# Regrouping the TensorE steps of a sliding-window attention stage, with the zeroed keys made on GpSimd

## The chip, the cores and the metric

The kernel runs on one core of one Trainium2 chip. The metric is the device time of one execution in microseconds (us). An execution of this kernel was also profiled; its lines are quoted as the profile has them.

## The reference

A block of three stages on x of shape (8, 512, 512) in float32: x plus half of a gated feed-forward network of layernorm(x), then x plus attention of layernorm(x), then the feed-forward step again. The change lies in the attention. It has 32 heads of 16 columns, and a query sees its own position and the 128 before it:

```
q, k, v = heads(x @ Wq.T), heads(x @ Wk.T), heads(x @ Wv.T)
scores = einsum('bhnrd,bhncd->bhnrc', qb, kw) * scale      # blocks of 128 queries, 256 keys
scores = where(valid, scores, finfo.min)                   # 0 <= dist <= 128, no key before 0
out = einsum('bhnrc,bhncd->bhnrd', softmax(scores), vw)
return out @ Wo.T
```

The softmax subtracts each query's largest visible score before it exponentiates, and the kernel does so too.

## The kernel before, in words

The kernel has three stages, one after the other: feed-forward "a" (`ffn_stage`), attention (`attention_stage`, tiles with "_b"), feed-forward "c". Tiles of rows pass between them through DRAM (`rows_a`, `rows_b`).

**Units.** The attention is cut into 128 units. Unit u stands for one row b of the batch (8), one group i of 8 heads (4 per row, j = i mod 4; i runs from 0 to 31) and one block t of 128 positions (4 per group). So a row has 16 units and a group four, t = 0 to 3. Eight heads of 16 columns fill 128 partitions, in four strips g of 32 partitions with two heads h in each.

**Steps of a unit, by function, line and tile name:**

- `probabilities` (L510): transposed scores, keys against queries, into four PSUM tiles `sp` (L519), one for each strip, as matmuls on 32 of TensorE's rows. Each tile is 128 x 512 with both heads and 256 queries, at t = 3 half as wide. The keys come from `kz`, two copies of the keys in each of which one head's columns are zero and one column is 1, and the queries carry minus the maximum in the matching column. Each tile is then clamped at zero into `pT` in SBUF, three of them by ScalarE (L532) and the last, g = 3, by VectorE (L528); ScalarE exponentiates the whole (L534), and GpSimd zeroes what lies outside the window (`affine_select`, L539).
- `weighted` (L545), one unit later: probabilities times values into PSUM tile `av` (L555), on 32 of TensorE's columns, 32 matmul instructions, 16 at t = 0. After every second unit ScalarE copies it to `ab` (L564).
- `turned` (L566), after every second unit: four transposes of `ab` to `abT` (L573), then on VectorE the reciprocal of the sums (L576) and four multiplications to `o` (L580).
- `turned_back` (L587): two transposes `oTp` (L592), copied to `oT` by ScalarE (L595).
- `maxima` (L475), six units ahead (AHEAD): scores once more, queries against keys, into four PSUM tiles `sm` (L487), 128 wide at t = 0 and 256 else; VectorE masks each and takes its largest, eight reductions (L496) into `negs`.
- `subtract` (L501), once per group: four transposes `neg` (L505), and two operations on VectorE (L508) that put the maxima into the queries.
- one product per unit of 128 x 512, eight matmul instructions at L431: `values` (wv, t = 0, for the next row; evacuated by VectorE, L467), `output` (wo, t = 1, for the row before; it adds the residual `xr`, L601 to L607), `queries` (wq, t = 2) and `keys` (wk, t = 3), both three groups ahead, evacuated by ScalarE (q: L449 and L450; k: L457; `kz`: L459 and L460).
- `norm` of row b + 2 (L174): its load by `row_loaded`, statistics, scaled rows `xn`, and four transposes `ptn` (L205), copied to `xs` by ScalarE (L213).

**Buffers.** `ps_s` has five PSUM banks, taken in turn by `sp` and `sm` tiles, so that a group of four tiles takes one bank that has been free and the first three banks of the group before. `ps_mm` has two, taken in turn by products and by all transposes; `ps_av` has one. `pT` has three buffers.

**Order.** The loop over u at the end of `attention_stage` is the order in which TensorE, VectorE and ScalarE take the attention's instructions (`manual_schedule`). On TensorE a unit is: `sp`, half of the product, (`neg`, or `abT` at odd u), `sm`, the product's other half, (`ptn`), `av`, (`oTp`). `sum_of_products` returns a function that is called once for each half:

```
            if product:
                product()
...
            if product:
                product()
```

GpSimd and SyncE aren't ordered by hand. SyncE issues the loads and stores, ScalarE the stores of the feed-forward stages.

Of the kernel before, what the change touches and what calls it, by code (L numbers as in the profile page):

```python
# [8 lines left out]
F32 = mybir.dt.float32  # L9
# [15 lines left out]
def macaron_block(  # L25
# [147 lines left out]
    def norm(xnpool, xspool, psum, tag, xt, split, name):  # L173
# [9 lines left out]

        def statistics(_=0):
            for t in range(TB):
                st = small.tile([P, 6], F32, tag="st", name=f"st_{name}_{t}")
                nc.vector.bn_stats(st, xt[:, t, :])
                nc.vector.bn_aggr(mv[:, t, :], st)
            var = small.tile([P, TB], F32, tag="nvar", name=f"var_{name}")
            nc.vector.tensor_scalar(var, mv[:, :, 1], LN_EPS, None, ALU.add)  # L190
            inv_sqrt(rstd, var)

# [95 lines left out]
    def ffn_stage(kind, source, target, first):  # L288
        with ExitStack() as s:
# [25 lines left out]
            def prepare(b):  # L315
                xts[b] = xpool.tile([P, TB, D], F32, tag="x", name=f"x_{kind}{b}")
                nc.sync.dma_start(xts[b], source(b))
                xss[b], statistics, scaled, transposed = norm(
                    xnpool, xspools[b % 2], ps_tr, "tr", xts[b], True, f"{kind}{b}"
                )  # L320
                with tc.high_priority() if b == 0 else nullcontext():
                    statistics()
                    for t in range(TB):
                        scaled(t)
                        transposed(t)
# [44 lines left out]
    def attention_stage():  # L370
# [42 lines left out]

        qs, ks, kz, pTs, avs, abs_, os_, oTs = {}, {}, {}, {}, {}, {}, {}, {}
        NJ = DC
# [5 lines left out]
        def sum_of_products(name, pairs, done):  # L421

            half = len(pairs) // 2
            box = []

            def part():
                first = not box
                if first:
                    box.append(ps_mm.tile([P, T], F32, tag="mm", name=name))
                for n in range(0 if first else half, half if first else len(pairs)):  # L430
                    nc.tensor.matmul(  # L431
                        box[0], *pairs[n], start=(n == 0), stop=(n == len(pairs) - 1)
                    )
                if not first:
                    done(box[0])

            return part

        def project(w, b, j, done):
            cols = slice(j * P, (j + 1) * P)  # L440
            pairs = [(attn_w[w][:, k, cols], xss[b][:, k, :]) for k in range(DC)]
            return sum_of_products(f"{w}_{b}_{j}", pairs, done)

        def queries(i):
            return project("wq", i // NJ, i % NJ, lambda ps: queries_kept(i, ps))

# [5 lines left out]
        def keys(i):  # L452
            return project("wk", i // NJ, i % NJ, lambda ps: keys_kept(i, ps))

        def keys_kept(i, ps):
            ks[i] = ring.tile([P, T], F32, tag="k", name=f"k_{i}", bufs=3)
            nc.scalar.copy(ks[i], ps)  # L457
            kz[i] = [ring.tile([P, T], F32, tag=f"kz{h}", name=f"kz{h}_{i}") for h in range(2)]
            nc.scalar.activation(kz[i][0], ps, AF.Identity, scale=half0, bias=at16)  # L459
            nc.scalar.activation(kz[i][1], ps, AF.Identity, scale=half1, bias=at0)  # L460

        def values(b, t):
            rows = slice(t * P, (t + 1) * P)
            pairs = [(xss[b][:, k, rows], attn_w["wv"][:, k, :]) for k in range(DC)]
            return sum_of_products(
                f"wv_{b}_{t}", pairs,
                lambda ps: nc.vector.tensor_copy(  # L467
                    vones[b % 2][:, t, :, :DK], ps.rearrange("p (h d) -> p h d", d=DK)
                ),
            )  # L470
# [39 lines left out]
        def probabilities(u):  # L510
# [14 lines left out]
            for g in range(NG):  # L525
                under = pT[:, 2 * g : 2 * g + 2, : n * P]
                if g == NG - 1:
                    nc.vector.tensor_scalar(  # L528
# [37 lines left out]
        def turned(u):  # L566

            i, t = u // TB, u % TB
            pt = ps_mm.tile([P, 2, 2, P], F32, tag="mm", name=f"abT_{u}")
            ab = abs_.pop(i)  # L570
            for m in range(2):
                for h in range(2):
                    nc.tensor.transpose(pt[:, m, h, :], ab[:, h, m, :], ident)  # L573
            rows = pt.rearrange("p m h (g r) -> p (m h) g r", r=32)
            rden = small.tile([P, 4, NG, 1], F32, tag="rden", name=f"rden_{u}")
# [9 lines left out]
        def turned_back(u):  # L585
# [11 lines left out]
            )  # L597

        def output(b, t):
            xr = work.tile([P, D], F32, tag="xr", name=f"xr_{b}_{t}")  # L600
            nc.sync.dma_start(xr, rows_a[b][:, t, :])  # L601
            rows = slice(t * P, (t + 1) * P)
# [5 lines left out]

            return sum_of_products(f"wo_{b}_{t}", pairs, done)

        AHEAD = 6
        row = NJ * TB
        engines = {mybir.EngineType.PE, mybir.EngineType.DVE, mybir.EngineType.Activation}
        s.enter_context(tc.manual_schedule(engines=engines))
        for u in range(-row - row // 2 - 2, units + row):
            i, t = u // TB, u % TB
            b, j = i // NJ, i % NJ
            if j == 1 and t == 2 and 0 < b + 2 < B:
                row_loaded(b + 2)
            if b == -2 and j == 2:  # L620
                with tc.high_priority():
                    for part in norms[0] if t == 0 else norms[0][1:]:
                        part(t)
            if j == 2 and t == 0 and 0 < b + 2 < B:
                norms[b + 2][0]()
            if 0 <= u < units:
                probabilities(u)
            product = None
            if b == -1 and j >= 2 and t < 2:
                product = values(0, 2 * (j - 2) + t)  # L630
            if t == 0 and 0 < b + 1 < B:
                product = values(b + 1, j)
            if t == 1 and 0 <= b - 1 < B:
                product = output(b - 1, j)
            if t == 2 and 0 <= i + 3 < B * NJ:
                product = queries(i + 3)
            if t == 3 and 0 <= i + 3 < B * NJ:
                product = keys(i + 3)
            if product:
                product()  # L640
            if j == 2 and 0 < b + 2 < B:
                norms[b + 2][1](t)
            if 0 <= u - 1 + AHEAD < units and (u - 1 + AHEAD) % TB == TB - 1:
                subtract((u - 1 + AHEAD) // TB)
            if 0 <= u - 2 < units and (u - 2) % 2 == 1:
                turned(u - 2)
            if 0 <= u + AHEAD < units:
                maxima(u + AHEAD)
            if product:
                product()  # L650
            if j == 2 and 0 < b + 2 < B:
                norms[b + 2][2](t)
            if 0 <= u - 1 < units:
                weighted(u - 1)
            if 0 <= u - 2 < units and (u - 2) % 2 == 1:
                turned_back(u - 2)
        s.close()

# [31 lines left out]
```

## Time and profile before

| | us |
|---|---|
| median of 3 runs | 2540.91 |
| lowest, highest | 2538.38, 2542.39 |
| the profiled execution's own time | 2538.64 |
| its span in the profile | 2536.9 |
| TensorE busy (PE) | 2446.1 |
| VectorE busy (DVE) | 1300.1 |
| ScalarE busy (ACT) | 1024.5 |
| GpSimd busy (POOL) | 895.5 |

In the profile PE is TensorE's matmuls and PEld its weight loads, which overlap them. A line of the timeline has the start in us, the length in us, the engine, the line of the kernel, the operation, output <- inputs, their shapes, how often, and in square brackets how long the engine was idle before it and what ended that. Matmuls are pipelined: their ends overlap the next step's start, so what a step costs is read from start to start. A matmul of float32 is two instructions in the profile, so `sp` shows as x16 and half a product as x4. A stretch line has from:to and length, then busy time and instructions of PE, PEld, DVE, ACT and POOL, the granted clock, the DMA share and GB/s. The feed-forward stages take the time up to about 829 us and from about 1803 us on; the units of the attention begin with the first `sp` at 877.0 us.

### The profile page before, as it was taken

The numbers are of one execution on the slowest core, as the hardware profiler recorded it, in microseconds if no ns is written. First come the engines' busy times: TensorE is split into PE (matmuls) and PEld (weight loads), VectorE is DVE, ScalarE is ACT, GpSimd is POOL, SyncE is SP. The second block draws the span as 40 slices with busy tenths as digits, with TensorE's granted clock in tenths as the row PEclk, the third lists the DMA queues.
The fourth block names the chain that finished last, engine by engine and source line by source line (L and its number), as shares of the span: only waits on it lengthen the run. The fifth ranks groups of instructions, "written<-read, shape, count | busy, mean of one in ns | idle before, by whom it ended". The sixth has DMA issues, their size and how long they took to land.

```text
span 2536.9 us, 40366 instructions
## 1 busy us (share of the span) xinstructions
PE 2446.1 (96%) x16184; PEld 1755.5 (69%) x16184; DVE 1300.1 (51%) x3785; ACT 1024.5 (40%) x1524; POOL 895.5 (35%) x742
## 2 busy tenths in 40 slices
PE   5789999999999999999999999999999999999998
PEld 4668888888888455555555555555688888888887
DVE  7774434434434465656665666666334433443433
ACT  6762222222222366666566565556322222222221
POOL 0004444444445132222222222223344444444444
PEclk9999999999999999999999999999999999999999
DMA  4431000000011000101010000013400000000000
GB/s 149 149 133 46 34 15 20 34 34 1 34 67 67 34 2 26 35 18 35 22 37 20 18 18 18 18 55 114 137 18 17 34 34 1 34 34 1 34 17 17
DMA packets 38907, 103.25 MB, mean 41 GB/s; under 512 B 2880, under 2 KB 6976, under 8 KB 35648
## 3 DMA queue, kind: packets, MB, share of 16 engines
q1 hardware_dynamic: 33344, 83.90, 9.6%
q10 hardware_dynamic: 5376, 16.78, 1.7%
q8 instruction: 127, 2.08, 0.3%
q14 instruction: 60, 0.49, 0.1%
HBM read 62.91 MB, written 37.75 MB: 40 GB/s over the span
## 4 chain that ended last, share of the span: by engine, by line
PE 90%; DVE 6%; ACT 2%; issue 1%; DMA 0%; POOL 0%; DVEq 0%; POOLq 0%; ACTq 0%; SPq 0%
PE gu_c L233 18%; PE gu_a L233 18%; PE o_c L266 9%; PE o_a L266 8%; PE sm L487 5%; PE sp L519 5%; PE wq L431 5%; PE wk L431 5%; PE wv L431 5%; PE wo L431 4%; PE av L555 4%; PE abT L573 1%; PE oTp L592 1%; DVE xn_a L197 1%; PE neg L505 1%
## 5 line engine op out<-in xcount | busy, mean ns | idle before, releaser
L233 PE MATMUL gu_a<-xs_a,wgu_a 128*128 128x512 f32 x2048 | 503.4, 398 | 14.8 <-ACT wgu_a L153 14.8
L233 PE MATMUL gu_c<-xs_c,wgu_c 128*128 128x512 f32 x2048 | 489.0, 391 | 0.0
L539 POOL TENSOR_SCALAR_AFFINE_SELECT pT<-pT 128x1024 f32<-128x1024 f32 x224 | 239.9, 1091 | 650.5 <-ACT pT L534 650.5
L233 PEld LDWEIGHTS gu_a<-xs_a,wgu_a 128*128 128x128 f32 x2048 | 388.7, 192 | 97.5 <-ACT wgu_a L153 17.4
L233 PEld LDWEIGHTS gu_c<-xs_c,wgu_c 128*128 128x128 f32 x2048 | 383.0, 188 | 78.7
L496 DVE CUSTOM_DVE_ANT_0 seen<-sm,window 128x256 f32<-128x256 f32 (+1 forms) x1024 | 330.9, 387 | 75.9 <-PE sm L487 66.8
L266 PE MATMUL o_a<-wp_a,hs_a 128*128 128x512 f32 x1024 | 254.0, 391 | 5.9 <-ACT wp_a L153 5.9
L266 PE MATMUL o_c<-wp_c,hs_c 128*128 128x512 f32 x1024 | 251.5, 389 | 0.0
L241 DVE TENSOR_TENSOR h_c<-gu_c,sg_c 128x512 f32<-128x512 f32 x128 | 88.5, 691 | 293.8 <-PE gu_c L233 291.5
L259 POOL TENSOR_TENSOR sq_c<-h_c 128x512 f32<-128x512 f32 x120 | 124.8, 1040 | 323.5 <-DVE h_c L241 309.8
L266 PEld LDWEIGHTS o_a<-wp_a,hs_a 128*128 128x128 f32 x1024 | 191.0, 188 | 46.9 <-ACT wp_a L153 7.8
L534 ACT ACTIVATE pT<-pT 128x2048 f32<-128x2048 f32 (+1 forms) x128 | 217.2, 1697 | 12.1 <-DVE pT L528 8.4
L266 PEld LDWEIGHTS o_c<-wp_c,hs_c 128*128 128x128 f32 x1024 | 192.3, 188 | 39.8
L241 DVE TENSOR_TENSOR h_a<-gu_a,sg_a 128x512 f32<-128x512 f32 x128 | 88.4, 691 | 256.0 <-PE gu_a L233 254.6
L259 POOL TENSOR_TENSOR sq_a<-h_a 128x512 f32<-128x512 f32 x105 | 109.7, 1045 | 276.5 <-DVE h_a L241 265.1
L532 ACT ACTIVATE pT<-sp 128x512 f32<-128x512 f32 (+1 forms) x384 | 181.2, 545 | 57.9 <-PE sp L519 57.9
L260 POOL TENSOR_TENSOR ss_c<-ss_c,sq_c 128x512 f32<-128x512 f32 x120 | 191.7, 1598 | 8.9
L239 ACT ACTIVATE sg_c<-gu_c 128x512 f32<-128x512 f32 x128 | 76.6, 598 | 270.2 <-PE gu_c L233 270.1
L243 ACT CAST hs_c<-h_c 128x512 fp32r<-128x512 f32 x128 | 79.6, 622 | 254.7 <-DVE h_c L241 254.7
L239 ACT ACTIVATE sg_a<-gu_a 128x512 f32<-128x512 f32 x128 | 76.6, 598 | 257.7 <-PE gu_a L233 257.7
L243 ACT CAST hs_a<-h_a 128x512 fp32r<-128x512 f32 x128 | 79.6, 622 | 225.2 <-DVE h_a L241 225.2
L260 POOL TENSOR_TENSOR ss_a<-ss_a,sq_a 128x512 f32<-128x512 f32 x105 | 167.6, 1596 | 7.8
(129 smaller groups left out, 3041.0 us busy)
## 6 DMA issues: line engine op xcount, KB each, us to landing
x_a<-x_dram SPq DMA_DIRECT2D x8, 1024.0 KB, 5.4
wf_gu<-w_gate_up_dram SPq DMA_DIRECT2D x16, 512.0 KB, 3.6
wgu_kept<-wgu_a SPq DMA_DIRECT2D x16, 512.0 KB, 2.8
rows_a<-x_a ACTq DMA_DIRECT2D x8, 1024.0 KB, 3.9
xr<-rows_a SPq DMA_DIRECT2D x32, 256.0 KB, 3.1
x_b<-rows_a SPq DMA_DIRECT2D x8, 1024.0 KB, 4.8
rows_b<-xr SPq DMA_DIRECT2D x32, 256.0 KB, 2.4
x_c<-rows_b SPq DMA_DIRECT2D x8, 1024.0 KB, 4.8
```

What stands on the lines that cost most here:

```text
L233: nc.tensor.matmul(ps, wgu[c][:, i * DC + k, :], xs[:, s, k, :], start=(k == 0 and s == 0), stop=(k == DC - 1 and s == 1),)
L239: nc.scalar.activation(sg, gu[0], AF.Silu)
L241: nc.vector.tensor_tensor(h, gu[1], sg, ALU.mult)
L243: nc.scalar.copy(hs[c][:, 0, :], h)
L259: nc.gpsimd.tensor_tensor(sq, h, h, ALU.mult)
L260: nc.gpsimd.tensor_tensor(sumsq, sumsq, sq, ALU.add)
L266: nc.tensor.matmul(ops[t], ht[:, s, t * P : (t + 1) * P], wp[e // 2][:, e % 2, :], start=(e == 0 and s == 0), stop=(e == FC - 1 and s == 1),)
L431: nc.tensor.matmul(box[0], *pairs[n], start=(n == 0), stop=(n == len(pairs) - 1))
L496: nc.vector.tensor_tensor_reduce(out=seen[:, : n * P], in0=tiles[g][:, h, : n * P], in1=window[:, (2 - n) * P :], scale=-1.0, scalar=3.4e3 ...
L532: nc.scalar.activation(under, tiles[g][:, :, : n * P], AF.Relu, scale=-1.0)
L534: nc.scalar.activation(seen, seen, AF.Exp, scale=-1.0)
L539: nc.gpsimd.affine_select(out=half, in_=half, compare_op=ALU.is_ge, fill=0.0, base=0, pattern=[[0, 2 * NG], [sign, P]], channel_multiplier ...
```

## The change

- The product of a unit is no longer cut in halves: `sum_of_products` issues all of it.
- The order of a unit on TensorE becomes: `sp`, `av` of the unit before, `sm`, (`neg`), the whole product, (`ptn`), then `abT` at even u and `oTp` at odd u. `turned` keeps the transposes, one unit earlier than before; its VectorE part becomes `divided`, which stands right after `probabilities`.
- The clamp that VectorE does is that of strip g = 1 in place of the last.
- The two `kz` tiles of a group are made by GpSimd from `k` in SBUF, one in each of the two units that follow `keys`, in place of by ScalarE from PSUM. GpSimd's order is now set by hand too.
- The residual rows are loaded one unit ahead of `output`, by ScalarE's queue in place of SyncE's.
- `row_loaded` stands at the end of j = 0, t = 3 in place of j = 1, t = 2, and the norm's statistics are spread over the four units of j = 1. On VectorE the norm's scaling now stands behind the unit's maxima.

```diff
@@ -181,14 +181,14 @@
         mv = small.tile([P, TB, 2], F32, tag="mv", name=f"mv_{name}")
         rstd = small.tile([P, TB], F32, tag="nrstd", name=f"rstd_{name}")
 
-        def statistics(_=0):
-            for t in range(TB):
-                st = small.tile([P, 6], F32, tag="st", name=f"st_{name}_{t}")
-                nc.vector.bn_stats(st, xt[:, t, :])
-                nc.vector.bn_aggr(mv[:, t, :], st)
-            var = small.tile([P, TB], F32, tag="nvar", name=f"var_{name}")
-            nc.vector.tensor_scalar(var, mv[:, :, 1], LN_EPS, None, ALU.add)
-            inv_sqrt(rstd, var)
+        def statistics(t):
+            st = small.tile([P, 6], F32, tag="st", name=f"st_{name}_{t}")
+            nc.vector.bn_stats(st, xt[:, t, :])
+            nc.vector.bn_aggr(mv[:, t, :], st)
+            if t == TB - 1:
+                var = small.tile([P, TB], F32, tag="nvar", name=f"var_{name}")
+                nc.vector.tensor_scalar(var, mv[:, :, 1], LN_EPS, None, ALU.add)
+                inv_sqrt(rstd, var)
 
         xns = {}
 
@@ -411,7 +412,8 @@
         for tile_ in negs:
             nc.gpsimd.memset(tile_, 0.0)
 
-        qs, ks, kz, pTs, avs, abs_, os_, oTs = {}, {}, {}, {}, {}, {}, {}, {}
+        later, xrs = [], {}
+        abTs, qs, ks, kz, pTs, avs, abs_, os_, oTs = {}, {}, {}, {}, {}, {}, {}, {}, {}
         NJ = DC
         units = B * NJ * TB
 
@@ -419,30 +421,18 @@
             return u // TB // NJ, u // TB % NJ, u % TB
 
         def sum_of_products(name, pairs, done):
-
-            half = len(pairs) // 2
-            box = []
-
-            def part():
-                first = not box
-                if first:
-                    box.append(ps_mm.tile([P, T], F32, tag="mm", name=name))
-                for n in range(0 if first else half, half if first else len(pairs)):
-                    nc.tensor.matmul(
-                        box[0], *pairs[n], start=(n == 0), stop=(n == len(pairs) - 1)
-                    )
-                if not first:
-                    done(box[0])
-
-            return part
+            ps = ps_mm.tile([P, T], F32, tag="mm", name=name)
+            for n, (lhs, rhs) in enumerate(pairs):
+                nc.tensor.matmul(ps, lhs, rhs, start=(n == 0), stop=(n == len(pairs) - 1))
+            done(ps)
 
         def project(w, b, j, done):
             cols = slice(j * P, (j + 1) * P)
             pairs = [(attn_w[w][:, k, cols], xss[b][:, k, :]) for k in range(DC)]
-            return sum_of_products(f"{w}_{b}_{j}", pairs, done)
+            sum_of_products(f"{w}_{b}_{j}", pairs, done)
 
         def queries(i):
-            return project("wq", i // NJ, i % NJ, lambda ps: queries_kept(i, ps))
+            project("wq", i // NJ, i % NJ, lambda ps: queries_kept(i, ps))
 
         def queries_kept(i, ps):
             qs[i] = [ring.tile([P, T], F32, tag=f"q{h}", name=f"q{h}_{i}") for h in range(2)]
@@ -450,19 +440,22 @@
             nc.scalar.activation(qs[i][1], ps, AF.Copy, scale=scale1)
 
         def keys(i):
-            return project("wk", i // NJ, i % NJ, lambda ps: keys_kept(i, ps))
+            project("wk", i // NJ, i % NJ, lambda ps: keys_kept(i, ps))
 
         def keys_kept(i, ps):
             ks[i] = ring.tile([P, T], F32, tag="k", name=f"k_{i}", bufs=3)
             nc.scalar.copy(ks[i], ps)
-            kz[i] = [ring.tile([P, T], F32, tag=f"kz{h}", name=f"kz{h}_{i}") for h in range(2)]
-            nc.scalar.activation(kz[i][0], ps, AF.Identity, scale=half0, bias=at16)
-            nc.scalar.activation(kz[i][1], ps, AF.Identity, scale=half1, bias=at0)
+            kz[i] = {}
+            later.extend([(i, 0, half0, at16), (i, 1, half1, at0)])
+
+        def keys_of_head(i, h, kept, at):
+            kz[i][h] = ring.tile([P, T], F32, tag=f"kz{h}", name=f"kz{h}_{i}")
+            nc.gpsimd.tensor_scalar(kz[i][h], ks[i], kept, at, ALU.mult, ALU.add)
 
         def values(b, t):
             rows = slice(t * P, (t + 1) * P)
             pairs = [(xss[b][:, k, rows], attn_w["wv"][:, k, :]) for k in range(DC)]
-            return sum_of_products(
+            sum_of_products(
                 f"wv_{b}_{t}", pairs,
                 lambda ps: nc.vector.tensor_copy(
                     vones[b % 2][:, t, :, :DK], ps.rearrange("p (h d) -> p h d", d=DK)
@@ -524,7 +517,7 @@
 
             for g in range(NG):
                 under = pT[:, 2 * g : 2 * g + 2, : n * P]
-                if g == NG - 1:
+                if g == 1:
                     nc.vector.tensor_scalar(
                         under, tiles[g][:, :, : n * P], -1.0, 0.0, ALU.mult, ALU.max
                     )
@@ -566,12 +559,15 @@
         def turned(u):
 
             i, t = u // TB, u % TB
-            pt = ps_mm.tile([P, 2, 2, P], F32, tag="mm", name=f"abT_{u}")
+            pt = abTs[i] = ps_mm.tile([P, 2, 2, P], F32, tag="mm", name=f"abT_{u}")
             ab = abs_.pop(i)
             for m in range(2):
                 for h in range(2):
                     nc.tensor.transpose(pt[:, m, h, :], ab[:, h, m, :], ident)
-            rows = pt.rearrange("p m h (g r) -> p (m h) g r", r=32)
+
+        def divided(u):
+            i, t = u // TB, u % TB
+            rows = abTs.pop(i).rearrange("p m h (g r) -> p (m h) g r", r=32)
             rden = small.tile([P, 4, NG, 1], F32, tag="rden", name=f"rden_{u}")
             nc.vector.reciprocal(rden, rows[:, :, :, DK : DK + 1])
             os_[i] = work.tile([P, 2, NG, 2, DK], F32, tag="o", name=f"o_{u}", bufs=2)
@@ -596,9 +592,12 @@
                 oTs[i][:, (t - 1) * P : (t + 1) * P], back.rearrange("p m q -> p (m q)")
             )
 
+        def residual_loaded(b, t):
+            xrs[b, t] = work.tile([P, D], F32, tag="xr", name=f"xr_{b}_{t}")
+            nc.scalar.dma_start(xrs[b, t], rows_a[b][:, t, :])
+
         def output(b, t):
-            xr = work.tile([P, D], F32, tag="xr", name=f"xr_{b}_{t}")
-            nc.sync.dma_start(xr, rows_a[b][:, t, :])
+            xr = xrs.pop((b, t))
             rows = slice(t * P, (t + 1) * P)
             pairs = [(oTs[NJ * b + j][:, rows], attn_w["wo"][:, j, :]) for j in range(NJ)]
 
@@ -606,54 +605,60 @@
                 nc.vector.tensor_tensor(xr, ps, xr, ALU.add)
                 nc.sync.dma_start(rows_b[b][:, t, :], xr)
 
-            return sum_of_products(f"wo_{b}_{t}", pairs, done)
+            sum_of_products(f"wo_{b}_{t}", pairs, done)
 
         AHEAD = 6
         row = NJ * TB
-        engines = {mybir.EngineType.PE, mybir.EngineType.DVE, mybir.EngineType.Activation}
+        engines = {
+            mybir.EngineType.PE, mybir.EngineType.DVE, mybir.EngineType.Activation,
+            mybir.EngineType.Pool,
+        }
         s.enter_context(tc.manual_schedule(engines=engines))
         for u in range(-row - row // 2 - 2, units + row):
             i, t = u // TB, u % TB
             b, j = i // NJ, i % NJ
-            if j == 1 and t == 2 and 0 < b + 2 < B:
-                row_loaded(b + 2)
             if b == -2 and j == 2:
                 with tc.high_priority():
-                    for part in norms[0] if t == 0 else norms[0][1:]:
+                    if t == 0:
+                        for block in range(TB):
+                            norms[0][0](block)
+                    for part in norms[0][1:]:
                         part(t)
-            if j == 2 and t == 0 and 0 < b + 2 < B:
-                norms[b + 2][0]()
             if 0 <= u < units:
                 probabilities(u)
-            product = None
-            if b == -1 and j >= 2 and t < 2:
-                product = values(0, 2 * (j - 2) + t)
-            if t == 0 and 0 < b + 1 < B:
-                product = values(b + 1, j)
-            if t == 1 and 0 <= b - 1 < B:
-                product = output(b - 1, j)
-            if t == 2 and 0 <= i + 3 < B * NJ:
-                product = queries(i + 3)
-            if t == 3 and 0 <= i + 3 < B * NJ:
-                product = keys(i + 3)
-            if product:
-                product()
-            if j == 2 and 0 < b + 2 < B:
-                norms[b + 2][1](t)
+            if 0 <= u - 2 < units and (u - 2) % 2 == 1:
+                divided(u - 2)
+            if later:
+                keys_of_head(*later.pop(0))
+            if 0 <= u - 1 < units:
+                weighted(u - 1)
+            if t == 0 and 0 <= b - 1 < B:
+                residual_loaded(b - 1, j)
+            if 0 <= u + AHEAD < units:
+                maxima(u + AHEAD)
+            if j in (1, 2) and 0 < b + 2 < B:
+                norms[b + 2][j - 1](t)
+
             if 0 <= u - 1 + AHEAD < units and (u - 1 + AHEAD) % TB == TB - 1:
                 subtract((u - 1 + AHEAD) // TB)
-            if 0 <= u - 2 < units and (u - 2) % 2 == 1:
-                turned(u - 2)
-            if 0 <= u + AHEAD < units:
-                maxima(u + AHEAD)
-            if product:
-                product()
+            if b == -1 and j >= 2 and t < 2:
+                values(0, 2 * (j - 2) + t)
+            if t == 0 and 0 < b + 1 < B:
+                values(b + 1, j)
+            if t == 1 and 0 <= b - 1 < B:
+                output(b - 1, j)
+            if t == 2 and 0 <= i + 3 < B * NJ:
+                queries(i + 3)
+            if t == 3 and 0 <= i + 3 < B * NJ:
+                keys(i + 3)
             if j == 2 and 0 < b + 2 < B:
                 norms[b + 2][2](t)
-            if 0 <= u - 1 < units:
-                weighted(u - 1)
+            if 0 <= u - 1 < units and (u - 1) % 2 == 1:
+                turned(u - 1)
             if 0 <= u - 2 < units and (u - 2) % 2 == 1:
                 turned_back(u - 2)
+            if j == 0 and t == 3 and 0 < b + 2 < B:
+                row_loaded(b + 2)
         s.close()
 
     ffn_stage("a", lambda b: tokens(x, b), lambda b: rows_a[b], True)
```

More of the change, by code (lines that the diff above doesn't have):

```diff
@@ L321, in prepare @@
                 with tc.high_priority() if b == 0 else nullcontext():
-                    statistics()
+                    for t in range(TB):
+                        statistics(t)
                     for t in range(TB):
```

## The prediction

> **What bounds the kernel now.** I read the page's busy shares first, then the busy time by stretch, then TensorE's timeline of a steady group, then the one place where TensorE is seen to wait for score banks.
>
> ```profile
> PE 2446.1 (96%) x16184; PEld 1755.5 (69%) x16184; DVE 1300.1 (51%) x3785; ACT 1024.5 (40%) x1524; POOL 895.5 (35%) x742
> ...
> PE 90%; DVE 6%; ACT 2%; issue 1%; DMA 0%; POOL 0%; DVEq 0%; POOLq 0%; ACTq 0%; SPq 0%
> ```
>
> TensorE carries nine tenths of the chain. By stretch (length, then busy time of PE, PEld, DVE, ACT, POOL):
>
> ```profile
> 1341.10:1459.10 118.00, 116.83 (x1169) 64.23 (x1168) 73.67 (x341) 71.44 (x106) 30.99 (x29) 1.00 0.06 19
> 1577.10:1692.10 115.00, 115.00 (x1156) 62.25 (x1155) 68.59 (x328) 69.30 (x102) 29.98 (x28) 1.00 0.06 20
> ```
>
> These are two rows b (16 units each) of the attention stage, the only stage the change touches in time: rows take 118.0 us with the norm of a later row inside, 115.0 without. TensorE never rests in the second. Two units (t = 2, then the start of t = 3) on TensorE:
>
> ```profile
> 1355.48 1.15 PE L519 MATMUL sp<-q,kz 32*128 32x256 f32 x16
> 1356.56 1.99 PE L431 MATMUL wq<-xs_b,wq_sb 128*128 128x512 f32 x4
> 1358.38 0.60 PE L505 MATMUL neg<-ident,negs 128*128 128x128 f32 x4
> 1358.91 0.73 PE L487 MATMUL sm<-k,q 32*128 32x128 f32 x16
> 1359.57 1.98 PE L431 MATMUL wq<-xs_b,wq_sb 128*128 128x512 f32 x4
> 1361.48 1.08 PE L555 MATMUL av<-pT,vones_sb 128*32 128x128 f32 x32
> 1362.49 0.73 PE L519 MATMUL sp<-q,kz 32*128 32x128 f32 x16
> ```
>
> The cost of a step is start to start: sp 1.08, half a product 1.82 before a transpose and 1.91 before a tiled step, sm 0.66 (128 wide; 1.08 at 256), av 1.01 (0.57 at t = 1), and from the other units abT 0.53, oTp 0.37. Each repeats within 0.01 us. So the question is what the new order costs TensorE, and whether a wait opens that the half product between sp and sm covers today. What that wait looks like is seen at the start, where for once no product stood between them:
>
> ```profile
> 883.48 1.33 PE L519 MATMUL sp<-q,kz 32*128 32x256 f32 x16
> ...
> 884.70 1.58 ACT L532 ACTIVATE pT<-sp 128x512 f32<-128x512 f32 x3 [1.02 <-PE sp L519]
> 884.85 0.69 DVE L528 TENSOR_SCALAR pT<-sp 128x512 f32<-128x512 f32 x1
> 885.35 0.29 PEld L487 LDWEIGHTS sm<-k,q 32*128 32x128 f32 x2 [0.69 <-ACT pT L532]
> ...
> 885.84 0.29 PEld L487 LDWEIGHTS sm<-k,q 32*128 32x128 f32 x2 [0.20 <-ACT pT L532]
> ...
> 886.33 0.72 PEld L487 LDWEIGHTS sm<-k,q 32*128 32x128 f32 x10 [0.20 <-ACT pT L532]
> ...
> 887.39 0.65 PE L555 MATMUL av<-pT,vones_sb 128*32 128x128 f32 x16
> ```
>
> Five score banks rotate through groups of four tiles, so sm's tiles 1, 2, 3 need the banks of sp's tiles 0, 1, 2. ScalarE's three clamps (L532) free them 1.87, 2.36 and 2.85 us after sp's start; after the last, TensorE needs 1.06 us more.
>
> [...] The trace agrees, at about 0.1 us a change (1.91 against 1.82 above; a product entered from a tiled step costs 0.11 more than one entered from a transpose). [...]
>
> **The change part by part.**
>
> 1. *Fewer mode changes, whole products.* New order: sp, av, sm, (neg), product of eight, (ptn), abT or oTp. A whole product is 8 x 0.43 + 0.11 = 3.54 us (3.43 behind neg). Without waits:
> t0: 1.08 + 1.01 + 1.08 + 3.54 + 0.53 = 7.23 (now 6.99);
> t1: 1.08 + 0.57 + 1.08 + 3.54 + 0.37 = 6.63 (7.36);
> t2: 1.08 + 1.01 + 0.66 + 0.44 + 3.43 + 0.53 = 7.14 (7.01), 0.44 being neg with no mode change behind it;
> t3: 0.66 + 1.01 + 1.08 + 3.54 + 0.37 = 6.65 (7.38).
> Sum 27.65 against 28.74, or 1.09 us less for each of 32 groups: -35 us, if nothing waits. sp before av in place of a product costs the same 0.30 us from its last matmul, seen twice in the tail.
>
> 2. *The cover of the clamps shrinks.* Between sp and sm stands only av. The fourth clamp, on VectorE, moves from tile 3 to tile 1, so ScalarE's second clamp now frees tile 2's bank: at 2.36, with VectorE's done near 2.05 (start 1.36 when idle, 0.69 long). In t0 and t2, sm starts at 1.08 + 1.01 = 2.09 and the next step begins at 2.36 + 1.06 = 3.42 in place of 3.17: 0.25 lost (0.26 at t2). In t1 av is half as long: 3.42 in place of 2.73, 0.69 lost. In t3 the tiles are half as wide (ScalarE's second clamp ends at 1.46, sm would start at 1.67): nothing. Together 1.20 a group, +38 us. So groups end at 7.48, 7.32, 7.40, 6.65 = 28.85: +0.11 each, or +3.5 us in all. What hides the rest: the next sp needs sm's first three tiles read, six reductions of 0.34 from 3.1, so by 5.2, and comes at 7.3; av needs the selects of the unit before, done 6.95 after its sp (exp ends 4.74, two selects of 1.09), and comes 8.4 after it. At t2 abT takes neg's bank, freed when VectorE has done maxima and subtraction, near 6.0; it is wanted at 6.9.
>
> 3. *Transposes behind the product, two accumulation banks.* ps_mm has two banks, so in the norm's row j = 2, (product, ptn, abT/oTp), the last takes the product's own bank and waits for its evacuation. From the product's last matmul: k copied at 1.22, both q at 1.9, values and output sum on VectorE at about 1.35, each + 0.05; the transpose wants to start at 0.43 + 0.44 = 0.87. Waits 0.5 (t0), 0.5 (t1), 1.08 (t2), 0.4 (t3) = 2.5 a row. Today oTp waits there too, in t1 and t3, for 1.3 together (8.46 in place of 7.80 and 7.82). Net +1.2 for five full rows, and with part 2: 5 x 1.6 = +8. Row 0 lacks the output product, and its norm's ptn then waits for VectorE's maxima, which now precede it: +1.7. Row 6: +0.4.
>
> 4. *Zeroed keys to GpSimd.* ScalarE loses 64 x 0.78 = 50 us, none on the path but the t3 wait counted in part 3. GpSimd gains 64 operations, each between half the select of 1024 (0.55) and the two-input operation of 512 (1.04); I take 1.0. The next select behind it is over 4 us away and the keys are used more than two groups later. No cost; with that cover gone, 64 x 1.0 at most.
>
> 5. *Moved loads and statistics.* The residual load goes from SyncE's queue to ScalarE's (32 issues, ahead of use by a unit; landing 3.1 us); behind it on ScalarE stand copies and clamps, 2 us or more away. x_b is issued earlier and its statistics are spread over four units of VectorE (0.85 each, inside the 0.9 us left at t2 and more elsewhere). Between nothing and 32 x 0.32 = 10 us if ScalarE held the issue time; I take nothing.
>
> 6. *Tail.* Units without a product: abT now follows av at once and waits for ScalarE's clamps, exp and copy (5.3 after sp), so about 5.9 where 2.1 to 5.1 is seen; odd units gain 0.8 to 1.3 from whole products. +4, within -4 and +10. Start-up: nothing, within 3 either way.
>
> Sum on the profiled execution (span 2536.9, its time 2538.6): +8 + 1.7 + 0.4 + 4 = +14, so 2552.6. The median of the runs shown is 2540.9, 2.3 above that execution, so I predict 2555. About 0.2% (5 us) is what a measurement of this kernel can tell from no change.
>
> **The rivals.** *A, faster:* the clamps do not hold sm up. It decides at one place, sm's last bank: if it is free 1.65 us after sp's start, the 38 us of part 2 vanish and the grouping's 35 us stay: 2555 - 38 = 2517. For it: today no steady sm waits, and VectorE now takes a middle tile. Against: the start-up lines, where each bank is released by its clamp, at a time set by sp's own end. *B, more slower:* clamps come later than in the start-up since ScalarE still has q or oT copies, or VectorE the values' copy, at sp's end: 0.3 us in three units of each group is 32 x 0.9 = 29: 2584. For it: ScalarE ends its second q copy close to the t3 clamps. Against: it ends by 0.9 and these start at 0.80. *C, no difference:* parts 3 and 6 are hidden: 2540.9 + 3.5 = 2544. That the change doesn't do what it says is excluded: the built order shows the new grouping and these waits.
>
> **How the numbers follow.** Forecast 0.57 (2546 to 2566, the bank waits known to 0.1 us, the tail to 6), A 0.17, B 0.13, C 0.13. Eight in ten needs forecast, C and most of B: 2537 to 2584. Faster 0.17, same (2536 to 2546) 0.13, slower 0.70.
>
> **What would show it.** Group starts at 7.48, 7.32, 7.40, 6.65 and rows near 115.4 and 119.6; sm waiting for ScalarE's pT in t0, t1, t2 and not in t3; abT behind the q copy in j = 2. Wrong if sm's last bank is free before av ends, or if av waits for GpSimd in steady rows.

## The result, and the profile after

The changed kernel takes 2560.8 us (median of 4 runs, 2557.4 to 2563.6) against 2539.6 us of the kernel before in the same comparison (4 runs, 2538.0 to 2542.4): a ratio of 1.0082, with a 95% interval of 1.0064 to 1.0099. It is slower by 21 us; the forecast was slower by 14. The profiled execution of the changed kernel took 2563.55 us, with a span of 2561.5, which is 24.6 more than the span before.

On the page of the changed kernel, the engines' busy time and the shares of the chain:

```profile
PE 2452.0 (96%) x16184; PEld 1792.2 (70%) x16184; DVE 1310.7 (51%) x3785; ACT 977.0 (38%) x1460; POOL 948.5 (37%) x806
...
PE 88%; DVE 7%; ACT 3%; issue 1%; DMA 1%; POOL 0%; DVEq 0%; POOLq 0%; ACTq 0%; SPq 0%
```

TensorE is still the bound, with the same 16184 matmuls. Its busy time rose by 6 us although the new order has fewer mode changes, as the forecast calls the switches between tiled steps (`sp`, `sm`, `av`) and whole matmuls (in the trace of before, half a product costs 1.91 us in front of a tiled step and 1.82 in front of a transpose). A wait that falls inside a group of matmuls is counted as the group's time (`sm` below: 0.25 us of 0.91), and so is work at a lower clock, which comes in below. ScalarE gave up 64 instructions and 47.5 us, GpSimd took 64 instructions and 53 us.

The same two rows by stretch, one with a norm inside (b = 4) and one without (b = 6):

```profile
1351.05:1470.94 119.89, 118.28 (x1173) 69.72 (x1172) 75.28 (x341) 65.46 (x97) 37.64 (x37) 1.00 0.06 19
1591.08:1706.28 115.20, 115.20 (x1157) 68.37 (x1156) 68.65 (x328) 63.15 (x93) 36.14 (x36) 1.00 0.07 20
```

They were 118.0 and 115.0. The same unit t = 2 and the start of t = 3 on TensorE's timeline:

```profile
1394.57 1.15 PE L512 MATMUL sp<-q,kz 32*128 32x256 f32 x16
1395.65 1.08 PE L548 MATMUL av<-pT,vones_sb 128*32 128x128 f32 x32
1396.66 0.98 PE L480 MATMUL sm<-k,q 32*128 32x128 f32 x16
1397.57 0.66 PE L498 MATMUL neg<-ident,negs 128*128 128x128 f32 x4
1398.07 3.60 PE L426 MATMUL wq<-xs_b,wq_sb 128*128 128x512 f32 x8
...
1402.13 0.73 PE L512 MATMUL sp<-q,kz 32*128 32x128 f32 x16
```

The narrow `sm` takes 0.91 us from its start to `neg`, where it took 0.66: the other 0.25 is a wait for a bank, inside the group. Unit t = 1 shows it best, because there `av` is shortest (all engines, other lines left out):

```profile
1358.51 1.15 PE L512 MATMUL sp<-q,kz 32*128 32x256 f32 x16
1359.58 0.65 PE L548 MATMUL av<-pT,vones_sb 128*32 128x128 f32 x16
1359.73 1.57 ACT L525 ACTIVATE pT<-sp 128x512 f32<-128x512 f32 x3 [3.49 <-PE sp L512]
...
1360.16 1.84 PE L480 MATMUL sm<-k,q 32*128 32x256 f32 x16
...
1361.92 1.55 PE L426 MATMUL wo<-wo_sb,oT 128*128 128x512 f32 x3
```

ScalarE's three clamps start 1.22 us after `sp`; the second, which frees the last bank, ends at 2.31. `sm` starts at 1.65, stops, and the product begins at 3.41, where 2.73 was forecast without a wait.

Where the span's 24.6 us lie, from the first starts of `wq`, `sp` and the rows in both traces:

| stretch | before | after | forecast | measured |
|---|---|---|---|---|
| up to the first `wq` (the stage before) | 829.1 | 831.0 | 0 | +1.9 |
| first `wq` to first `sp` | 47.9 | 44.1 | 0 | -3.8 |
| row 0 | 110.2 | 116.2 | +1.7 | +6.1 |
| rows 1 to 5 | 590.0 | 599.8 | +8 | +9.7 |
| row 6 | 115.0 | 115.2 | +0.4 | +0.2 |
| row 7 to the last `wo` | 110.7 | 121.3 | +4 | +10.6 |
| the rest | 734.1 | 733.9 | 0 | -0.2 |

The steady rows are where the forecast put them. Row 0 and the tail are not, and this is what the wait in row 0 looks like on TensorE, in unit t = 1 of j = 2:

```profile
945.52 1.11 PE L205 MATMUL ptn_b<-ident,xn_b 128*128 128x128 f32 x4 [3.86 <-DVE xn_b L197]
...
947.00 2.09 PE L512 MATMUL sp<-q,kz 32*128 32x256 f32 x16
949.02 1.58 PE L548 MATMUL av<-pT,vones_sb 128*32 128x128 f32 x32
```

The norm's transposes `ptn` wait 3.86 us for VectorE's scaling, which now stands behind the maxima. And then everything is slow: `ptn` takes 1.11 us and not 0.66, `sp` 2.09 and not 1.15. The stretch view shows why (its third figure from the end is the granted clock):

```profile
942.00:945.50 3.50, 0.00 (x0) 0.00 (x0) 3.47 (x15) 0.91 (x1) 2.45 (x3) 0.68 0.00 0
945.50:950.00 4.50, 4.48 (x42) 3.28 (x46) 0.69 (x1) 1.69 (x4) 0.61 (x1) 0.50 0.00 0
```

After the idle stretch TensorE runs at half clock: granted clock 0.50, from inside the gap on and for 6.8 us. The forecast did not count this. In the records of the granted clock of both kernels every stretch below full speed is at 0.50, and all but the one that ends each record are 3.4 or 6.8 us long. In the changed kernel such a stretch also began inside gaps of 2.52 and 3.12 us (see the last section). From the first `sp` to the last output product these stretches sum to 6.8 us before and 23.9 us after.

### The profile page after: what moved, and what is told of

The parts are those of the page before. It is cut to its first block, busy times and chain, and to the rows that moved or that the text cites. A ratio compares the mean times of both kernels' runs of the same rounds, so it can differ in the third digit from the quotient of the medians.

```text
span 2561.5 us, 40354 instructions
## 1 busy us (share of the span) xinstructions
PE 2452.0 (96%) x16184; PEld 1792.2 (70%) x16184; DVE 1310.7 (51%) x3785; ACT 977.0 (38%) x1460; POOL 948.5 (37%) x806
## 4 chain that ended last, share of the span: by engine, by line
PE 88%; DVE 7%; ACT 3%; issue 1%; DMA 1%; POOL 0%; DVEq 0%; POOLq 0%; ACTq 0%; SPq 0%
PE gu_a L233 18%; PE gu_c L233 18%; PE o_c L266 8%; PE o_a L266 8%; PE sm L480 6%; PE sp L512 5%; PE wk L426 5%; PE av L548 4%; PE wq L426 4%; PE wo L426 4%; PE wv L426 4%; PE abT L566 1%; DVE seen L489 1%; PE neg L498 1%; PE oTp L588 1%
## 5 line engine op out<-in xcount | busy, mean ns | idle before, releaser
L521 DVE TENSOR_SCALAR pT<-sp 128x512 f32<-128x512 f32 (+1 forms) x128 | 80.0, 625 | 210.6 <-PE sp L512 202.1
L480 PE MATMUL sm<-k,q 32*128 32x256 f32 (+1 forms) x2048 | 171.1, 380 | 3.2 <-DVE pT L521 1.6
```

What stands on the lines that cost most here:

```text
L480: nc.tensor.matmul(tiles[g][:, h, : n * P], qs[i][h][r, t * P : (t + 1) * P], ks[i][r, at], start=True, stop=True,)
```

## The experiments

Theory T, after the comparison: the grouping saves what was forecast, `sm` gives it back waiting for its last score bank, and units without a product wait for the other engines' chain, and pay again through the half clock. Rivals: the units are set by something else (mode changes, the maxima, the selects), or the keys on GpSimd or the moved loads cost time. All ratios below are to the kernel before; the changed kernel's is 1.0082.

**clamp_last.** The bank's release is moved later, nothing else:

```
-                if g == 1:
+                if g == NG - 1:
```

> The changed kernel with one edit: VectorE clamps tile 3 again in place of tile 1, so that the bank of tile 2 waits for ScalarE's third clamp. Theory (sm waits for its last score bank, and this wait gives back what the grouping gained): that bank comes free at 2.80 us after sp's start in place of 2.31, so t0, t1 and t2 lose 0.49 us more each and t3 about 0.1: groups of 30.4 in place of 28.80, 48 us slower than the changed kernel (42 to 54). Rival (the units are set by TensorE's own steps, or by VectorE's maxima or GpSimd's selects): groups stay at 28.8 and the time within 3 us of the changed kernel.

Measured: 2606.7 us, ratio 1.0252 (1.0238 to 1.0266), so 1.7% or 43 us slower than the changed kernel. Units are 7.97, 7.75, 7.95 and 6.72: 30.39 a group, or +0.49, +0.48, +0.49 and +0.13. In unit t = 0:

```profile
1378.19 1.89 PE L480 MATMUL sm<-k,q 32*128 32x256 f32 x16
1380.01 3.70 PE L426 MATMUL wv<-wv_sb,xs_b 128*128 128x512 f32 x8
```

`sm` takes 1.82 from start to start where it took 1.33, and 1.08 without a wait. One clamp more ahead of the bank costs one clamp of ScalarE in each unit with wide tiles, and the time is lost inside `sm`: the release of that bank sets these units. The rival falls.

**filled.** The opposite: work is put in front of the wait. Transposes leave the end of the unit and go between `sp` and `av`, one unit later; the first two lines stand in `probabilities`, between the clamps and `exp`:

```
+            if 0 <= u - 3 and (u - 3) % 2 == 1:
+                turned_back(u - 3)
...
             if 0 <= u - 2 < units and (u - 2) % 2 == 1:
+                turned(u - 2)
                 divided(u - 2)
...
-            if 0 <= u - 1 < units and (u - 1) % 2 == 1:
-                turned(u - 1)
-            if 0 <= u - 2 < units and (u - 2) % 2 == 1:
-                turned_back(u - 2)
```

> The changed kernel with the transposes abT and oTp moved from behind the product to between sp and av, one unit later than now (oT's copy between ScalarE's clamps and its exp). Theory (the bank wait is idle TensorE time that any work ahead of sm fills, and late transposes cost nothing): sm starts after its last bank is free, and units come to 7.12, 6.96, 7.03 and 6.92 us (two more mode changes of 0.1 counted), 28.03 a group in place of 28.80, -25 us; abT in the units without a product no longer stands behind av of its own unit, -8 in the tail, and in j = 2 no transpose waits for the product's evacuation, -8: about 2520, 20 us faster than the kernel before. Rival 1 (the wait moves with it: abT or oTp now waits for VectorE's division or ScalarE's copies, or the product for a bank of ps_mm): units stay near 7.2 and the time near the changed kernel, 2555 to 2565. Rival 2 (the stall belongs to the mode changes, not to the banks): units grow by the moved transposes' own changes, slower than the changed kernel by some 10 us.

Measured: 2547.8 us, ratio 1.0021 (1.0011 to 1.0030): 0.6% or 16 us faster than the changed kernel, not the 40 expected. The steady part holds. TensorE's timeline, t = 1 and the start of t = 2:

```profile
1232.81 0.66 PE L568 MATMUL abT<-ident,ab 128*128 128x128 f32 x4
1233.39 0.64 PE L550 MATMUL av<-pT,vones_sb 128*32 128x128 f32 x16
1233.97 1.25 PE L480 MATMUL sm<-k,q 32*128 32x256 f32 x16
1235.15 3.70 PE L426 MATMUL wo<-wo_sb,oT 128*128 128x512 f32 x8
1238.78 1.15 PE L512 MATMUL sp<-q,kz 32*128 32x256 f32 x16
```

`sm` now costs 1.18, 0.10 of it wait, where it cost 1.76. Units are 7.16, 7.05, 7.14 and 6.96: 28.31 a group, 0.49 less than in the changed kernel and 0.43 less than before. The wait was idle time that could be filled. Part of the miss is that the units came out 0.28 a group above the sum, and that the units of j = 2 kept waits (8.06, 8.00, 8.39 and 7.43): in row 3 `ptn` waits 0.27, 0.32 and 0.63 us for VectorE at t = 0, 1 and 2. The rest is that row 0 grew (119.6 us against 116.2) and the last row stayed (120.5 against 121.3): without a product the next `sp` follows `sm` so soon that it waits for the maxima to free its banks, as here in row 0, and the half clock in the attention stage came to 41.0 us. The -8 expected of the tail was wrong.

```profile
908.29 1.25 PE L480 MATMUL sm<-k,q 32*128 32x256 f32 x16
909.26 0.59 PE L512 MATMUL sp<-q,kz 32*128 32x256 f32 x2
910.28 3.41 PE L512 MATMUL sp<-q,kz 32*128 32x256 f32 x14 [0.44 <-DVE negs L489]
```

**tail_old.** `abT` of the last row alone is put back where it was:

```
+            if units - row < u - 2 < units and (u - 2) % 2 == 1:
+                turned(u - 2)
...
-            if 0 <= u - 1 < units and (u - 1) % 2 == 1:
+            if 0 <= u - 1 < units - row and (u - 1) % 2 == 1:
                 turned(u - 1)
```

> The changed kernel with abT of the last row alone one unit later, as in the kernel before (right behind the next sp, with its division behind it). Theory (in units without a product abT follows av at once and waits for ScalarE's clamps, exp and copy): the last row falls from 121.3 to about 111 us between its first sp and its last output product, so 6 to 10 us faster than the changed kernel and nothing else moves. Rival (the last row is held by GpSimd's selects and VectorE's share of the next stage's statistics in any order): within 2 us of the changed kernel.

Measured: 2558.7 us, ratio 1.0062 (1.0049 to 1.0074), 5 us below the changed kernel by the ratios, with intervals that overlap. In the traces the last row with its outputs falls from 121.3 to 116.9. This stretch differs between executions: `xr_sync` and `scale_first`, whose last rows do the changed kernel's work in its order, took 119.4 and 119.8. So `abT` behind its own `av` is some 2.5 to 4.4 of the 10.6 us lost there: more than the rival allows, less than the theory asked. The half clock in the tail is 13.7 us in both and 6.8 before, worth 3.4 us of full-speed work. What is left was not taken apart.

**scale_first.** The norm's scaling goes back ahead of the maxima on VectorE:

```
+            if j == 2 and 0 < b + 2 < B:
+                norms[b + 2][1](t)
             if 0 <= u + AHEAD < units:
                 maxima(u + AHEAD)
-            if j in (1, 2) and 0 < b + 2 < B:
-                norms[b + 2][j - 1](t)
+            if j == 1 and 0 < b + 2 < B:
+                norms[b + 2][0](t)
```

> The changed kernel with the norm's scaling xn in units of j = 2 put ahead of the maxima on VectorE, where the kernel before has it, in place of behind them. Theory (in row 0, which has no output product, ptn waits 3.86 us for xn behind the maxima of its unit, and by 0.2 to 0.4 us elsewhere): row 0 falls by 4 to 6 us and rows 1 to 5 by 0 to 0.4 each, together 4 to 8 us faster than the changed kernel. Rival (xn ahead of the maxima delays these, and the next sp or the subtraction waits in its place): row 0 gains less than 2 us, or the other rows lose what it gains; within 3 us of the changed kernel.

Measured: 2556.9 us, ratio 1.0053 (1.0039 to 1.0066), 0.3% or 7 us below the changed kernel, with intervals that just overlap. Row 0 falls from 116.2 to 111.3; rows 1 to 5 by 0.06 each only. There the wait just moves on by one step: in row 3 `ptn` no longer waits for `xn` (0.17 at t = 0, 0.24 at t = 1), and the last transpose now waits for VectorE to evacuate the product instead (0.44 and 0.35). The place of the long wait in row 0, on TensorE:

```profile
941.88 0.66 PE L205 MATMUL ptn_b<-ident,xn_b 128*128 128x128 f32 x4
942.37 0.38 PE L588 MATMUL oTp<-ident,o 128*128 128x128 f32 x2
942.68 2.26 PE L512 MATMUL sp<-q,kz 32*128 32x256 f32 x16
```

```profile
945.50:950.00 4.50, 4.50 (x46) 2.55 (x36) 3.49 (x19) 3.08 (x4) 2.69 (x3) 1.00 0.00 0
```

The wait of 3.86 is gone, the clock is full, and row 0 gains 4.9. That is 1.0 more than the wait, although `sp` now waits for score banks itself (2.26).

**kz_scalar.** The changed kernel with the zeroed keys on ScalarE again:

```
-            kz[i] = {}
-            later.extend([(i, 0, half0, at16), (i, 1, half1, at0)])
+            kz[i] = [ring.tile([P, T], F32, tag=f"kz{h}", name=f"kz{h}_{i}") for h in range(2)]
+            nc.scalar.activation(kz[i][0], ps, AF.Identity, scale=half0, bias=at16)
+            nc.scalar.activation(kz[i][1], ps, AF.Identity, scale=half1, bias=at0)
```

> The changed kernel with one part undone: the zeroed keys kz made by ScalarE from PSUM again, right behind k's copy, in place of by GpSimd. Theory (moving them was worth little by itself but the new order needs it: with whole products the k copy ends late in t3, and two more copies of 0.78 us would end about 0.9 us after the next sp's clamps are due): t0 loses up to 0.9 us in each of 32 groups and the last transpose of t3 in j = 2 up to 1.5 us in each of six rows, 20 to 38 us slower than the changed kernel. Rival (as forecast: only the wait in t3 of j = 2 is on the path): 4 to 10 us slower. A third: no difference, within 2 us.

Measured: 2591.4 us, ratio 1.0195 (1.0181 to 1.0209), 29 us slower than the changed kernel. Units t = 0 take 8.25 in place of 7.48, and t3 of j = 2 takes 8.84 in place of 7.50. ScalarE at t = 0, whose `sp` starts at 1275.34:

```profile
1275.23 0.59 ACT L447 COPY k<-wk 128x512 f32<-128x512 f32 x1 [3.64 <-PE wk L426]
1275.71 0.78 ACT L449 ACTIVATE kz<-wk,at,half 128x512 f32<-128x512 f32 x1
1276.38 0.78 ACT L450 ACTIVATE kz<-wk,at,half 128x512 f32<-128x512 f32 x1
...
1277.30 1.60 ACT L522 ACTIVATE pT<-sp 128x512 f32<-128x512 f32 x3
```

The clamps start 1.96 us after `sp`, not 1.22, and `sm` passes the 0.74 on. This is the mechanism of rival B: once the bank wait is on the path, every copy on ScalarE ahead of the clamps is too.

**before_kz.** The kernel before with that part alone (`keys_of_head` and `later` as in the diff, GpSimd added to the engines of the written order):

> The kernel before with one part of the change alone: the zeroed keys kz made by GpSimd from k, one of the two in each of the two units that follow. Theory (it takes away the wait of oTp for ScalarE's kz in t3 of j = 2, some 0.6 us in each of seven rows, and up to 3.8 us of the start-up, which was that much shorter in the changed kernel; GpSimd has time for it): 4 to 8 us faster than the kernel before, rows 1 to 5 at 117.4 in place of 118.0. Rival (hidden anyway, or GpSimd's selects come later by it): within 2 us of the kernel before, and the short start-up belongs to the new order.

Measured: 2536.9 us, ratio 0.9979 (0.9972 to 0.9986), 5 us faster. Units t3 of j = 2 take 7.82 in place of 8.46 (0.64 in six rows, 3.9 us), the start-up 46.5 in place of 47.9. No other steady unit moves: in the old order the product covered the clamps.

**xr_sync.** The changed kernel with the residual loads issued by SyncE:

```
-            nc.scalar.dma_start(xrs[b, t], rows_a[b][:, t, :])
+            nc.sync.dma_start(xrs[b, t], rows_a[b][:, t, :])
```

> The changed kernel with the residual loads issued from SyncE again, in the place in the program that the change gave them. Theory (32 issues on ScalarE cost nothing that is on the path): within 2 us of the changed kernel. Rival (each issue holds ScalarE's next clamps by about 0.3 us in t0, where the bank wait is on the path): up to 10 us faster than the changed kernel.

Measured: 2561.6 us, ratio 1.0076 (1.0063 to 1.0089). No difference that can be told. In the changed kernel each issue stands behind the clamps, at `exp`'s start, so it holds nothing that releases a bank.

**combined.** `filled` and `scale_first` together, and products cut in two where the units lack one. In the core of it, `part(count)` issues the next `count` of a product's four matmuls:

```
+            cut = b == 0 and j != 2
...
+            if b == B - 1 and t < 2:
+                begun = product = output(b - 1, j) if t == 0 else begun
+                count = DC // 2
...
+            if cut and t in (1, 2) and 0 <= i + 3 < B * NJ:
+                begun = product = queries(i + 3) if t == 1 else begun
+                count = DC // 2
```

> The changed kernel with the transposes between sp and av (as in the run filled), the norm's scaling ahead of the maxima (as in scale_first), and products cut in two where units lack one: in row 0 (j other than 2) half of wq's product in t1 and half in t2, with neg behind it; in row 7 half of wo's in t0 and half in t1. Theory (in rows 0 and 7 units without a product leave TensorE waiting for the chain of clamps, exp and selects, and after such waits it runs at half clock for one or two stretches of 3.4 us; spreading the products takes both away): rows 1 to 5 at 116.8, row 6 at 113.2, row 0 near 104 in place of 116.2 and the last row to the last output product near 110 in place of 121: some 40 us faster than the changed kernel, 2515 to 2528. Rival (the chain of the other engines sets these units, with or without products in them): rows 0 and 7 stay within 3 us of the run filled with the gain of scale_first, about 2540.

Measured: 2516.9 us, ratio 0.9900 (0.9886 to 0.9914): 25 us faster than the kernel before and 46 faster than the changed kernel. A row with a norm (b = 3):

```profile
1212.60:1327.90 115.30, 115.04 (x1169) 64.90 (x1168) 74.12 (x341) 63.94 (x96) 37.06 (x37) 1.00 0.09 29
```

Row 0 takes 104.6 us, rows 1 to 5 115.3, row 6 113.2, the last row with its outputs 109.0. Rows 1 to 5 came out 1.5 below the expectation: with the transposes ahead of `av`, little behind `ptn` waits for the product's bank (0.26 us, in `abT` at t = 3), so the earlier scaling counts in all of them and not in row 0 alone. The rival, that the other engines' chain sets rows 0 and 7 however the products lie, falls for row 0 (119.6 to 104.6). For row 7 (120.5 to 109.0) it falls too, though 109.0 is barely under the 110.7 of the kernel before, and what follows the last output product took 3.2 us longer than there (737.3 against 734.1). The half clock went from row 0 (granted clock 1.00 from 877.5 to 982 us) but not from the last row, which has 10.2 us of it. What each of the three parts gives was not separated.

## Why the forecast held, and where it did not

*Step 1, whole products and fewer mode changes.* It holds where nothing waits: t3 takes 6.59 (forecast 6.65), `sp` to `av` is 1.08, a product 3.54. The waits inside `sm` (0.25, 0.68 and 0.25 at t = 0, 1 and 2) taken off the measured 28.80 leave 27.62 a group, and the forecast without waits was 27.65. `filled` has some of this gain in the clock time: its groups end 0.43 below the kernel before, 14 of the 35 us, with one mode change more a unit than the changed kernel (not two, as was expected of it: a product costs 3.63 to the next `sp` there and 3.54 to a transpose) and a little wait left.

*Step 2, the bank.* Units 7.48, 7.27, 7.46 and 6.59 (forecast 7.48, 7.32, 7.40, 6.65): 28.80 a group against 28.85. The waits are 1.18 a group against 1.20. Taking the release times from the one place of the old trace without a product in between was enough. `clamp_last` and `filled` show cause and size from both sides. Rival A fell here: `sm`'s last bank is free at 2.31, not at 1.65. Rival B did not occur: ScalarE is idle for about 0.5 us or more ahead of the clamps at t = 0, 1 and 2. At t = 0 step 4 is the reason, as `kz_scalar` shows.

*Step 3, transposes behind the product in j = 2.* Rows 1 to 5 take 119.9 to 120.1 (forecast 119.6), and row 6 115.2 (115.4). At t = 2 and 3 the last transpose waits for ScalarE's copies, as forecast; t = 2 in row 3:

```profile
1314.15 0.66 PE L566 MATMUL abT<-ident,ab 128*128 128x128 f32 x4 [0.92 <-ACT q L440]
```

At t = 0 and 1 the size was right (a unit grows by 1.07 and 1.05 over one of another j, where the forecast's figures give 0.94), but the place was not: `ptn` waits there for `xn` behind the maxima, which the forecast priced for row 0 alone. `scale_first` shows that the evacuation would have held the last transpose nearly as long. For row 0 the mechanism was right (its `ptn` waits for VectorE's maxima) and the size was not: the term "+1.7" measured +6.1, and j = 2 alone +6.0. In a unit without a product nothing hides the maxima; `ptn` waited 3.86, more than the whole term, and the half clock slowed what followed.

*Step 4, the keys.* One operation on GpSimd takes 0.80 us (bounds 0.55 and 1.04, taken 1.0) and costs nothing that shows: in `before_kz` no steady unit grew, as forecast. But "none on the path" was true of the old order only. In the new one the same copies on ScalarE would cost 29 us, so this part is not a side edit: without it the change would have come out near 2590.

*Step 5, moved loads and statistics.* For the loads, nothing, shown by `xr_sync`. The statistics were not tried alone.

*Step 6, the tail and the start-up.* The term "+4" measured +10.6, just outside its -4 to +10. One execution of each kernel doesn't settle by how much it was too small: from `before_kz` (112.7) to `xr_sync` (119.4), whose last rows have the old order and the new one, it is +6.7. The wait of `abT` is as described, but it lengthens as the tail goes on, and two of the waits are followed by half clock:

```profile
1780.18 1.11 PE L566 MATMUL abT<-ident,ab 128*128 128x128 f32 x4 [2.52 <-ACT ab L557]
...
1790.86 1.11 PE L566 MATMUL abT<-ident,ab 128*128 128x128 f32 x4 [3.12 <-ACT ab L557]
```

In both, `abT` takes 1.11 us in place of 0.66. Neither mis-sized term priced this half clock. The start-up fell by 3.8 where nothing was forecast. Most of that comes with the new order: with the keys on ScalarE it still takes 44.6 us in the new order (`kz_scalar`), and with the keys on GpSimd 46.5 in the old one (`before_kz`). The 1.9 us ahead of the attention are not the change's: there the half clock sums to 27.3 us in place of 23.9, and the first `wq` came between 827.2 and 833.4 us in the profiles of all these kernels, which do the same work up to there.

Rival C, that parts 3 and 6 are hidden, fell on rows 0 and 7. The steady units' +3.5 is a small difference of two large terms, -35 and +38; it came out right because both did (27.62 and 1.18 a group, above). The sum of the steps, +14, was right in sign and in its main term; rows 0 and 7 are 11.0 over it, and the other differences nearly cancel.

## What to carry to other kernels

Work that stands between a producer and the next user of its PSUM banks is a cover with a price, here waits of 1.18 us a group. Before moving it, find when each bank is freed, take that time from a place in the trace where the cover is absent, and ask what other work could stand there. When a wait comes onto the path, the engine that ends it becomes critical with everything queued ahead on it: here two copies a group on ScalarE cost 29 us. At the edges of a pipeline, where units have less work, look at the granted clock behind a TensorE wait of some microseconds too: in the changed kernel 6.8 us of half clock began inside each of the waits of 2.52, 3.12 and 3.86 us, and none at one of 3.11.

## What was not expected of the hardware

TensorE's granted clock fell to 0.50 in the middle of a busy kernel. From the first `sp` to the last output product it did so for 6.8 us in the kernel before, 23.9 in the changed one, 41.0 in `filled` and 10.2 in `combined` (and 3.4 more just behind). In the changed kernel it began inside gaps of 2.52, 3.12 and 3.86 us, but not at one of 3.11 us that ended at 1804.9. It also came without such a gap: in the changed kernel at 888.7 us, just behind an `sp` that had been waiting for banks in pieces of 0.4 us, and in `tail_old` at 1768.1 us, inside such an `sp`.

The length of the gap alone does not sort these cases. In the kernel before, too, two gaps of 1.71 us in front of `abT` had different sequels: behind the one that ended at 1780.5 us `abT` took 1.11 us, at half clock, and behind the one that ended at 1764.3 it took 0.66, at full clock. What decides stays open here, and so does why last rows with the same work took 119.4 to 121.3 us.
